# A four-layer graph network: row entries by distance, one-hot rows from TensorE, the attention's halves in banks of their own, and another order of the first pairs

## The chip, the cores and the metric

The kernel runs on one core of a Trainium2 chip. The metric is device time in microseconds (us) of one execution. The kernel before takes 883.4 us, the median of three runs (883.37 to 884.81).

The engines are named as in the profile: PE is TensorE's matmuls and PEld its weight loads, DVE is VectorE, ACT is ScalarE, POOL is GpSimd, and SP is SyncE, which here only issues DMAs. L12 means line 12 of the kernel before.

## The reference

The input `x` is 32 batch items of 512 nodes with 128 features, and `adj` is a 512 x 512 matrix in which about an eighth of the entries are non-zero. Four layers follow each other, each of them a layer norm, a relu, a graph layer, and a residual addition:

```python
# layer 0
h = relu(layernorm(x))
h0, h1 = h @ W[0], h @ W[1]
m = adj > 0
idx = cumsum(m.reshape(-1)) - 1            # number of the entry in row-major order
A = softmax(where(m, e[0][idx], NEG), axis=1)
x = x + (A * I) @ h0 + (A * (1 - I)) @ h1 + bias
# layer 1: Chebyshev hops (h A, 2 (h A) A - h) with A = adj, twice, then relu(cat @ Theta1 + b1)
# layer 2: (adj * adj)^T relu(h psi), phi1 with relu, phi2
# layer 3: A = exp(8 tanh(h q (h k)^T / (8 sqrt(128)))) * adj, rows normalised, A @ h @ v
```

The table `e` has 256 values, and an index beyond it takes the last of them. Only the first 256 entries of `adj`, which lie in its first few rows, therefore have a value of their own; all later ones share `e[255]`. The change lies wholly in layer 0.

## The kernel before

**Tiling.** A tile has 128 partitions (P). The 512 nodes are NT = 4 blocks t of 128. The batch is worked in 16 pairs q of two items b. NE = 256 entries of the table are NK = 2 blocks kk of 128. The kernel has eight PSUM banks of 128 x 512 f32, which `bank()` (L84) hands out in turn; a new use of a bank waits until the readers of the last one are done. For PE, DVE, ACT and POOL the kernel is traced with a manual schedule: each engine runs its instructions in the order of the program text, and only semaphores tie the engines together. So where a line stands among the lines of the same engine is where it runs. The Python generators in the text (`early_stats`, `normed_steps`, `turn_steps`, `project_steps`) give out one piece of work at each `next` or `go`, by which the pieces of one pair are woven in between those of others.

**The front end (L186 to L715)** makes the attention matrix A, while TensorE has little else to do.

- Masks `m` and the counts `rc` of each row come from DVE (L519), the additive mask `att` from POOL (L521). `p_incl` (L545) is the running count up to and with each row.
- Row entries (L553 to L560): for each block t, `of_row[row, e]` is 1 where entry e of the table falls in that row. DVE makes it as two compares: `lt` is e < incl, and `of_row` is (e >= before) times `lt`. TensorE sums it against `m` into `p_row` (L558).
- Place of each entry: `p_known` (L565) gives for each entry the row that it lies in and the count before that row; `p_upto` (L602) and the DVE compare with a sum, `scr_c` (L616), give its column.
- One-hot matrices of 0, 1 and values over (entry, node), which DVE makes by comparing `cols` with a column of numbers: `at_row` (L619), `at_col` (L620), and `at_part` (L623, the table's values split in three bf16 parts).
- `score_rows(t)` (L651): two matmuls subtract the first 256 entries from the mask (`p_later`), and six put their values into `p_val`.
- `softmax_rows(t)` (L663): DVE adds the mask (L665), reduces (L667), ACT takes the exponential (L668). `scaled_rows(t)` (L674): ACT scales by the reciprocal sum, POOL cuts out the diagonal (`diag`, L678) and subtracts it (L679, writes `att`).
- The attention is transposed by TensorE, `transpose_rows` (L482, shown as L485), into four banks `pt[j]`, one per block j of source nodes, where the target blocks t = 0, 1 are the first half of columns, and 2, 3 the second. `att_high`, `att_low`, `att_mid` (L372 to L391) split each half into three parts of 128 x 256 for the fp32r matmuls, one instruction for each j.

**A pair of layer 0** needs: statistics (`bn_stats` on DVE, then four small POOL instructions for pairs 0 to 2), eight relus `h` on ACT (L313), the turning of h to features-by-nodes `hT` (pairs 0 to 2 by TensorE, L331 and L596, and an ACT copy; from pair 3 on by DVE `hb`, L349, and a round of DMAs through DRAM), the product `p_g` with W[1] (L446, called from L455 on in `project_steps`) and its split g_high (ACT, L468), g_low (DVE, L470), g_mid (POOL L474 or DVE L472), and `hd`, hT times the diagonal of A (POOL, L728). Then TensorE adds, in two banks per pair: `own_sums` (L793, 16 matmuls with `hd`) and `mixed(q, I, part)` (L800, 48 matmuls in six groups of eight).

**Order around the change.** `first_sums()` (L810 to L858) weaves pair 0's sums with the turning, product and `hd` of pair 1, and with the turning of pair 2. `round0(q)` (L862) runs pairs 1 to 15: own sums, the product of pair q + 1, three mixed groups, the turning of pair q + 3, and three mixed groups. With q = 2 the split of pair 3's product (`go(steps)`, with g_low on DVE) stands after the first mixed groups and ahead of `turn(5)`.

Of the kernel before, what the change touches and what calls it, by code (L numbers as in the profile page):

```python
# [29 lines left out]
def kernel(  # L30
# [174 lines left out]
    known = prep.tile([P, NT, 2], F16, name="known")  # L205
    nc.vector.tensor_copy(known[:, :, 1], rows)
# [160 lines left out]
    def of_half(j, half):  # L367

        cols_of = slice(half * H, half * H + H)
        return pt[j][:, cols_of], [part[:, j, cols_of] for part in att_parts]  # L370
# [9 lines left out]
    def att_low(half):  # L380

        for j in range(NT):
            p, (high, low, mid) = of_half(j, half)
            nc.vector.tensor_sub(low, p, high.bitcast(F32))

    def att_mid(half):

        for j in range(NT):
# [61 lines left out]
    def bias(q):  # L450

        for b in range(2):
# [29 lines left out]
    def transpose_rows(banks, src, t):  # L482

        for j in range(NT):
            nc.tensor.transpose(banks[j][:, blk(t)], src[:, t, blk(j)], ident)  # L485
# [38 lines left out]

    pi = bank("p_incl")
# [16 lines left out]
    incl = prep.tile([P, NT], F32, name="incl")  # L542
    nc.vector.tensor_copy(incl, pi[:, :NT])
    before = prep.tile([P, NT], F32, name="before")
    nc.vector.tensor_sub(before, incl, rc)  # L545
# [6 lines left out]
    for t in range(NT):  # L552
        s = prep.tile([P, NE], F16, tag="lt", name=f"lt_{t}", bufs=2)  # L553
        nc.vector.tensor_scalar(s, cols[:, :NE], incl[:, t : t + 1], None, OP.is_lt)
        nc.vector.scalar_tensor_tensor(of_row[:, t, :], cols[:, :NE], before[:, t : t + 1], s,
                                       OP.is_ge, OP.mult)
# [4 lines left out]
    nc.vector.tensor_scalar(known[:, :, 0], before, float(NE), None, OP.min)  # L561
    pb = bank("p_known")[:, : 2 * NK].rearrange("p (k e) -> p k e", e=2)
    for kk in range(NK):
        for t in range(NT):
            nc.tensor.matmul(pb[:, kk, :], of_row[:, t, blk(kk)], known[:, t, :],  # L565
# [5 lines left out]
    row_of = prep.tile([P, NK], F32, name="row_of")  # L571
    nc.vector.tensor_copy(row_of, pb[:, :, 1])
    rest = prep.tile([P, NK], F32, name="rest")
    nc.vector.tensor_sub(rest, rows[:, :NK], pb[:, :, 0])
# [25 lines left out]
    for kk in range(NK):  # L600
        for j in range(NT):
            nc.tensor.matmul(pw[kk][:, j * P :], pgs[:, j, blk(kk)], upto[:, j, j * P :],  # L602
                             start=(j == 0), stop=(j == NT - 1), skip_group_check=True)
    turn_first(0)
    p_qk = bank("p_qk")
# [4 lines left out]
    at_row = prep.tile([P, NK, N], BF16, name="at_row")  # L610
# [7 lines left out]
    for kk in range(NK):  # L618
        nc.vector.tensor_scalar(at_row[:, kk, :], cols, row_of[:, kk : kk + 1], None, OP.is_equal)  # L619
# [89 lines left out]
    for j in range(NT):  # L709
        att_high(j, 0, j >= 2)  # L710
# [820 lines left out]
```

## Time and profile before

The profiled execution took 883.62 us, of which 881.8 are its span; the mean granted clock of TensorE was 0.997.

| stretch, us | PE busy | DVE busy | ACT busy | POOL busy | clock | DMA share |
|---|---|---|---|---|---|---|
| 0 to 30 (front end) | 24.55 | 25.66 | 14.12 | 18.99 | 1.00 | 0.80 |
| 30 to 80 (pairs 0 to 5) | 48.47 | 38.03 | 35.05 | 38.26 | 0.97 | 0.36 |
| 80 to 240 | 159.33 | 116.34 | 83.10 | 124.67 | 1.00 | 0.42 |
| 240 to 480 | 240.00 | 191.55 | 144.03 | 173.62 | 1.00 | 0.27 |
| 480 to 881.8 | 397.82 | 330.80 | 298.38 | 252.88 | 1.00 | 0.48 |

| instruction, 0 to 80 us | engine | mean ns of one |
|---|---|---|
| row entries `of_row`, 128 x 256 f16 | DVE | 484 |
| reduction L667, 128 x 512 | DVE | 692 |
| exponential L668, 128 x 512 | ACT | 722 |
| scaling L675, 128 x 512 | ACT | 718 |
| `att_high`, 128 x 256 | ACT | 382 |
| `att_low`, `att_mid`, 128 x 256 | DVE | 415, 417 |
| relu `h`, 128 x 128 | ACT | 485 |
| `hd`, 128 x 512 | POOL | 1290 |
| power L236 | POOL | 1426 |

A row names the engine's busy time in a stretch, or the mean duration of one instruction of a kind. A busy share averages over all of a stretch: an engine that is busy for half of it can still be the one that another engine waits for, since each works through its own queue in order. Which engine that is shows in the waits, where each idle time of an engine is put down to the instruction whose semaphore came last.

### The profile page before, as it was taken

Reading aid. Unit: us, or ns where it says so; the run is one execution under the profiler, and the core shown is the slowest. Engines: PE = TensorE matmul, PEld = TensorE weight load, DVE = VectorE, ACT = ScalarE, POOL = GpSimd, SP = SyncE. Lnnn points to the kernel's source line nnn. Section 1 sums busy time; section 2 is a strip of 40 time slices with the busy share of each in tenths; the row PEclk is TensorE's granted clock in tenths of the full one; section 3 lists DMA queues with packets and bytes.
Section 4 is the critical chain, followed back from the end, with each engine's and each line's share of the span. In section 5 each row is a group of like instructions: output and inputs, shape, how many; then the busy total and the mean of one; then the engine's idle time right before and its main releaser. Section 6 shows DMA issues by size and latency. Waiting matters only on the chain.

```text
span 881.8 us, 16286 instructions
## 1 busy us (share of the span) xinstructions
PE 870.2 (99%) x5520; PEld 771.3 (87%) x5520; DVE 702.4 (80%) x1428; ACT 574.7 (65%) x1279; POOL 608.4 (69%) x624
## 2 busy tenths in 40 slices
PE   8999999999999999999999999999999999999998
PEld 4799999988888888888888888888889988899987
DVE  8769877568587787888778888888789789988875
ACT  4765565355555656556666888875688788766674
POOL 5768988766777867867776566565476766677664
PEclk9999999999999999999999999999999999999999
DMA  9146664312322213122342445455445555555433
GB/s 262 29 133 182 194 186 120 97 49 73 101 68 73 72 48 96 49 72 72 97 120 77 116 134 136 138 152 146 134 123 141 157 156 159 151 143 147 128 100 86
DMA packets 107684, 103.91 MB, mean 118 GB/s; under 512 B 9552, under 2 KB 94160, under 8 KB 107600
## 3 DMA queue, kind: packets, MB, share of 16 engines
q1 hardware_dynamic: 107312, 102.34, 41.1%
q8 instruction: 44, 0.72, 0.4%
q10 hardware_dynamic: 288, 0.52, 0.2%
q14 instruction: 40, 0.33, 0.1%
HBM read 53.02 MB, written 49.81 MB: 117 GB/s over the span
## 4 chain that ended last, share of the span: by engine, by line
PE 90%; DVE 3%; ACT 2%; POOL 2%; DMA 1%; issue 1%; SPq 0%; POOLq 0%; ACTq 0%; DVEq 0%
PE p_av L1298 13%; PE p_l L990 10%; PE p_hidden L1194 10%; PE p_x1T L397 10%; PE p_score L1276 10%; PE p_l L800 8%; PE p_w L969 5%; PE p_l L446 3%; PE p_z L446 3%; PE p_w L971 3%; PE p_feat L1171 3%; PE p_hidden L1174 3%; PE p_g L446 2%; PE p_query L1230 2%; PE p_hv L1242 2%; PE p_l L793 2%
## 5 line engine op out<-in xcount | busy, mean ns | idle before, releaser
L1298 PEld LDWEIGHTS p_av<-hv,ex 128*128 128x128 f32 x1024 | 119.2, 191 | 3.0 <-POOL ex L1271 0.4
L1298 PE MATMUL p_av<-hv,ex 128*128 128x129 f32 x1024 | 119.7, 274 | 0.2 <-POOL ex L1271 0.2
L313 ACT ACTIVATE h<-x,sh,rs 128x128 f32<-128x128 f32 x256 | 102.9, 483 | 4.4 <-POOL sh L260 2.3
L427 POOL TENSOR_TENSOR key<-key 128x512 fp32r<-128x512 f32 x32 | 47.9, 1498 | 83.4 <-DVE key L426 66.5
L1271 DVE TENSOR_TENSOR ex<-ex,adjTx 128x512 f32<-128x512 f32 x64 | 79.0, 1237 | 32.4 <-ACT ex L1269 31.0
L1271 POOL TENSOR_TENSOR ex<-ex,adjTx 128x512 f32<-128x512 f32 x64 | 99.6, 1574 | 6.9 <-issue 3.5
L1100 ACT ACTIVATE h<-x,sh,rs 128x128 f32<-128x128 f32 x256 | 102.9, 485 | 0.0
L413 POOL TENSOR_TENSOR low_h<-h,high_h 128x512 fp32r<-128x512 f32 x32 | 55.3, 1732 | 45.6 <-PE p_w L971 26.3
L1277 ACT ACTIVATE ex<-p_score 128x512 f32<-128x512 f32 x128 | 76.2, 598 | 11.5 <-PE p_score L1276 4.7
L1269 ACT ACTIVATE ex<-ex 128x512 f32<-128x512 f32 x128 | 77.3, 634 | 0.0
L1158 POOL TENSOR_SCALAR high_hT<-hT 128x512 fp32r<-128x512 f32 x32 | 20.5, 641 | 56.0 <-PE p_hidden L1174 28.9
L246 DVE BATCH_NORM_STATS2 bn<-x 128x6 f32<-128x256 f32 x160 | 58.3, 419 | 0.0
L399 ACT COPY x1T<-p_x1T 128x512 f32<-128x512 f32 x32 | 18.8, 587 | 57.7 <-PE p_x1T L397 57.7
L1214 POOL TENSOR_TENSOR x<-x,phi2b 128x256 f32<-128x256 f32 x64 | 56.3, 900 | 0.0
L413 POOL TENSOR_TENSOR low_hs<-hs,high_hs 128x512 fp32r<-128x512 f32 x32 | 44.0, 1388 | 14.9 <-ACT high_hs L412 14.4
L1276 PE MATMUL p_score<-high_query,key 128*128 128x512 f32 x128 | 50.5, 394 | 0.0
L1276 PE MATMUL p_score<-mid_query,key 128*128 128x512 f32 x128 | 50.4, 394 | 0.0
L1276 PE MATMUL p_score<-low_query,key 128*128 128x512 f32 x128 | 50.4, 394 | 0.0
L431 ACT ACTIVATE high_query<-p_query 128x512 fp32r<-128x512 f32 x32 | 19.2, 600 | 46.5 <-PE p_query L1230 46.5
L971 PE MATMUL p_w<-th,x1T 128*128 128x128 f32 x256 | 49.0, 273 | 0.0
L414 DVE SCALAR_TENSOR_TENSOR mid_h<-h,high_h 128x512 fp32r<-128x512 f32 x32 | 27.7, 870 | 23.7 <-ACT high_h L412 16.2
L1109 DVE STREAM_TRANSPOSE hb<-h 128x512 f32<-128x512 f32 x64 | 43.5, 697 | 2.5 <-DMA d<-hb 1.9
(246 smaller groups left out, 2623.1 us busy)
## 6 DMA issues: line engine op xcount, KB each, us to landing
d<-hb SPq DMA_DIRECT2D x128, 128.0 KB, 2.4
hT<-d SPq DMA_DIRECT2D x32, 512.0 KB, 3.7
d_hT<-hb_hT SPq DMA_DIRECT2D x116, 128.0 KB, 2.4
hT<-d_hT SPq DMA_DIRECT2D x29, 512.0 KB, 3.3
x<-in_x_dram SPq DMA_DIRECT2D x32, 256.0 KB, 5.3
dv<-hvb SPq DMA_DIRECT2D x128, 64.0 KB, 1.8
hvt<-dv SPq DMA_DIRECT2D x32, 256.0 KB, 2.7
out_dram<-x SPq DMA_DIRECT2D x31, 256.0 KB, 2.5
```

The source lines that it names most:

```text
L313: nc.scalar.activation(h[:, b, t, :], xt[q][:, b, t, :], AF.Relu, bias=shift[q][:, i : i + 1], scale=scale[q][:, i : i + 1])
L397: nc.tensor.matmul(p, right[part][:, blk(t)], left[part][:, t, :], start=(t == 0 and part == 0), stop=(t == NT - 1 and part == 2))
L413: nc.gpsimd.tensor_sub(low, x, high.bitcast(F32))
L971: nc.tensor.matmul(p[:, D:], x1[q, b][:, blk(t)], th[:, 2, :], start=False, stop=True, skip_group_check=True)
L990: nc.tensor.matmul(p, adj_parts[part][:, t, blk(i)], w[r][part][:, t, :], start=(part == 0 and t == 0), stop=(part == 2 and t == NT - 1))
L1100: nc.scalar.activation(h[:, t, :], xt[q][:, b, t, :], AF.Relu, bias=shift[q][:, i : i + 1], scale=scale[q][:, i : i + 1])
L1194: nc.tensor.matmul(sums2[n], weighed_features[n][i][:, blk(t)], sq[i][:, t, :], start=False, stop=(i == 2 and t == NT - 1), skip_group_che ...
L1269: nc.scalar.activation(ex[:, t, :], ex[:, t, :], AF.Exp, scale=8.0)
L1271: eng.tensor_mul(split(ex[:, t, :]), split(ex[:, t, :]), crossed(mask[:, t, :]))
L1276: nc.tensor.matmul(p, keys[n][i][:, t, :], query[n][i], start=(i == 0), stop=(i == 2))
L1277: nc.scalar.activation(crossed(ex[:, t, :]), split(p), AF.Tanh, scale=UP / (8.0 * math.sqrt(D)))
L1298: nc.tensor.matmul(po[:, i, : D + 1], ex[:, t, blk(i0 + i)], hv[:, t, :], start=(t == 0), stop=(t == NT - 1))
```

## The change

It does seven things.

1. Row entries by distance. A row holds entry e when e is less than half its count away from the middle of its span. POOL makes `half` and `above` from the counts, DVE one small subtraction `middle`; ACT takes the absolute distance to `middle` (Abs with a bias by partition) for each t, and DVE makes one compare in place of two. `before` is computed after the loop, and `known` has one column.
2. One-hot rows by TensorE. `row_places(kk)` turns `of_row` with four matmuls against a 16-bit identity, and ACT copies the result to `at_row`. The DVE compares for `at_row` and the copy `row_of` go. `p_known` writes into free columns of `p_incl`'s bank.
3. g_mid of the second item of pair 0 by DVE in place of POOL.
4. `score_rows` is split into `later_rows` and `value_rows`, which are issued in another order; the statistics of pair 1, the turning of pair 0's second item and `bias(0)` move among them, and the last scaling goes behind an `att_high`.
5. The transposed attention has two banks for each half: `pt[half][j]` holds the blocks 2j and 2j + 1 of one half, and the three splits work on 128 x 512 elements, two instructions for a half in place of four.
6. Another order in `first_sums`: p_adiag right after the second transposes, the own sums of pair 0 earlier, all eight relus of pair 2 ahead of the split of pair 1's product, and the own sums of pair 1 (`begun`) at its end, ahead of the turning of pair 2 (the first seam). `round0(1)` takes them over.
7. In `round0`, `turn(q + 3)` moves ahead of the q == 2 branch (the second seam).

```diff
-    known = prep.tile([P, NT, 2], F16, name="known")
-    nc.vector.tensor_copy(known[:, :, 1], rows)
+    known = prep.tile([P, NT], F16, name="known")
     upto = prep.tile([P, NT, N], F16, name="upto")
...
-        cols_of = slice(half * H, half * H + H)
-        return pt[j][:, cols_of], [part[:, j, cols_of] for part in att_parts]
+        rows_of, cols_of = slice(2 * j, 2 * j + 2), slice(half * H, half * H + H)
+        return (pt[half][j].rearrange("p (t c) -> p t c", t=2),
+                [part[:, rows_of, cols_of] for part in att_parts])
...
-        for j in range(NT):
+        for j in range(2):
             p, (high, low, mid) = of_half(j, half)
...
-        for j in range(NT):
+        for j in range(2):
             p, (high, low, mid) = of_half(j, half)
...
-        for b in range(2):
+        for b in (1, 0):
             nc.gpsimd.tensor_add(xt[q][:, b], xt[q][:, b], spread(b0, NT))
...
-    def transpose_rows(banks, src, t):
-
+    def transpose_rows(t):
+
+        half, i = divmod(t, 2)
         for j in range(NT):
-            nc.tensor.transpose(banks[j][:, blk(t)], src[:, t, blk(j)], ident)
+            place = (2 * (j % 2) + i) * P
+            nc.tensor.transpose(pt[half][j // 2][:, place : place + P], att[:, t, blk(j)], ident)
...
+    half = prep.tile([P, NT], F32, name="half")
+    nc.gpsimd.tensor_scalar(half, rc, 0.5, None, OP.mult)
+    above = prep.tile([P, NT], F32, name="above")
+    nc.gpsimd.tensor_scalar(above, rc, 0.5, 0.5, OP.mult, OP.add)
+
     pi = bank("p_incl")
...
     go(early[0], 2)
-    incl = prep.tile([P, NT], F32, name="incl")
-    nc.vector.tensor_copy(incl, pi[:, :NT])
-    before = prep.tile([P, NT], F32, name="before")
-    nc.vector.tensor_sub(before, incl, rc)
+    middle = prep.tile([P, NT], F32, name="middle")
+    nc.vector.tensor_sub(middle, above, pi[:, :NT])
     h = {q: normed_tile(q) for q in range(3)}
...
         s = prep.tile([P, NE], F16, tag="lt", name=f"lt_{t}", bufs=2)
-        nc.vector.tensor_scalar(s, cols[:, :NE], incl[:, t : t + 1], None, OP.is_lt)
-        nc.vector.scalar_tensor_tensor(of_row[:, t, :], cols[:, :NE], before[:, t : t + 1], s,
-                                       OP.is_ge, OP.mult)
+        nc.scalar.activation(s, cols[:, :NE], AF.Abs, bias=middle[:, t : t + 1])
+        nc.vector.tensor_scalar(of_row[:, t, :], s, half[:, t : t + 1], None, OP.is_lt)
         for j in range(NT):
...
     go(early[0], 2)
-    nc.vector.tensor_scalar(known[:, :, 0], before, float(NE), None, OP.min)
-    pb = bank("p_known")[:, : 2 * NK].rearrange("p (k e) -> p k e", e=2)
+    before = prep.tile([P, NT], F32, name="before")
+    nc.vector.tensor_sub(before, pi[:, :NT], rc)
+    nc.vector.tensor_scalar(known, before, float(NE), None, OP.min)
+    at_row = prep.tile([P, NK, N], BF16, name="at_row")
+
+    def row_places(kk):
+        p = bank(f"p_at_row_{kk}")
+        for t in range(NT):
+            nc.tensor.matmul(p[:, blk(t)], of_row[:, t, blk(kk)], ident16, start=True, stop=True)
+        return p
+
+    p_row_0 = row_places(0)
+    pb = pi[:, NT : NT + NK]
     for kk in range(NK):
         for t in range(NT):
-            nc.tensor.matmul(pb[:, kk, :], of_row[:, t, blk(kk)], known[:, t, :],
+            nc.tensor.matmul(pb[:, kk : kk + 1], of_row[:, t, blk(kk)], known[:, t : t + 1],
                              start=(t == 0), stop=(t == NT - 1))
...
     nc.vector.tensor_copy(pgs[:, 2:4, :], pg[1])
-    row_of = prep.tile([P, NK], F32, name="row_of")
-    nc.vector.tensor_copy(row_of, pb[:, :, 1])
+    nc.scalar.copy(at_row[:, 0, :], p_row_0)
     rest = prep.tile([P, NK], F32, name="rest")
-    nc.vector.tensor_sub(rest, rows[:, :NK], pb[:, :, 0])
+    nc.vector.tensor_sub(rest, rows[:, :NK], pb)
     go(normal[0], NT - 2)
...
                              start=(j == 0), stop=(j == NT - 1), skip_group_check=True)
+    p_row_1 = row_places(1)
     turn_first(0)
+    nc.scalar.copy(at_row[:, 1, :], p_row_1)
     p_qk = bank("p_qk")
...
     col_of = prep.tile([P, NK], F32, name="col_of")
-    at_row = prep.tile([P, NK, N], BF16, name="at_row")
     at_col = prep.tile([P, NK, N], BF16, name="at_col")
...
     for kk in range(NK):
-        nc.vector.tensor_scalar(at_row[:, kk, :], cols, row_of[:, kk : kk + 1], None, OP.is_equal)
         nc.vector.tensor_scalar(at_col[:, kk, :], cols, col_of[:, kk : kk + 1], -1.0, OP.is_equal, OP.mult)
...
         nc.vector.scalar_tensor_tensor(low, high.bitcast(F32), -LOW, pg, OP.mult, OP.add)
-        nc.gpsimd.tensor_sub(mid, high.bitcast(F32), low.bitcast(F32))
+        if b:
+            nc.vector.scalar_tensor_tensor(mid, high.bitcast(F32), LOW + 1.0, pg, OP.mult, OP.subtract)
+        else:
+            nc.gpsimd.tensor_sub(mid, high.bitcast(F32), low.bitcast(F32))
...
-    def score_rows(t):
-        ph = scores[t]
+    def later_rows(t):
         for kk in range(NK):
-            nc.tensor.matmul(ph, at_row[:, kk, blk(t)], at_col[:, kk, :], start=False, stop=(kk == NK - 1))
+            nc.tensor.matmul(scores[t], at_row[:, kk, blk(t)], at_col[:, kk, :], start=False, stop=(kk == NK - 1))
+
+    def value_rows(t):
         pv = bank(f"p_val_{t}")
...
                                  stop=(kk == NK - 1 and i == 2))
-        scores[t] = ph, pv
+        scores[t] = scores[t], pv
...
     squares = turn_adj()
-    score_rows(0)
+    later_rows(0)
+    later_rows(1)
+    value_rows(0)
     next(project[0][0])
+    bias(0)
     softmax_rows(0)
     go(project[0][0])
-    score_rows(1)
-    go(early[1], 1)
-    turn_first(1)
-    bias(0)
+    later_rows(2)
+    value_rows(1)
     softmax_rows(1, lambda: inverse(0))
     scaled_rows(0)
-    score_rows(2)
-    go(early[1], 2)
-    score_rows(3)
+    go(early[1], 1)
+    later_rows(3)
+    value_rows(2)
+    turn_first(1)
+    value_rows(3)
...
     next(project[0][1])
-    inverted(3)
-    pt = [bank(f"p_attT_{j}") for j in range(NT)]
-    transpose_rows(pt, att, 0)
-    transpose_rows(pt, att, 1)
-    for j in range(NT):
-        att_high(j, 0, j >= 2)
+    go(early[1], 1)
+    inverse(3)
+    pt = [[bank(f"p_attT_{half}_{j}") for j in range(2)] for half in range(2)]
+    transpose_rows(0)
+    transpose_rows(1)
+    att_high(0, 0, False)
+    att_high(1, 0, True)
+    scaled_rows(3)
+    go(early[1], 1)
     go(project[0][1])
...
+    begun = {}
+
     def first_sums():
...
         mixed(0, 0, ps[0], 0, True)
-        transpose_rows(pt, att, 2)
-        transpose_rows(pt, att, 3)
-        for j in range(NT):
-            att_high(j, 1, True)
-        go(normal[1])
-        go(early[2], NT + 2)
-        att_low(1)
-        att_mid(1)
-        mixed(0, 0, ps[0], 1, True)
-        mixed(0, 0, ps[0], 2, True)
+        transpose_rows(2)
+        transpose_rows(3)
         p_adiag = bank("p_adiag")
...
             nc.tensor.matmul(p_adiag[:, blk(t)], ones, diag[:, t, :], start=True, stop=True)
+        att_high(0, 1, True)
+        att_high(1, 1, True)
         nc.scalar.copy(adiag[0], p_adiag)
-        go(early[2])
         diagonal_of(0, 0)
         diagonal_of(0, 1)
+        go(normal[1])
+        mixed(0, 0, ps[0], 1, True)
+        mixed(0, 0, ps[0], 2, True)
+        mixed(0, 1, ps[1], 0, True)
+        att_low(1)
+        mixed(0, 1, ps[1], 1, True)
+        go(early[2])
+        att_mid(1)
         next(turned[1])
-        mixed(0, 1, ps[1], 0, True)
         go(turned[1])
-        go(normal[2], NT)
-        go(ln3, NT)
+        own_sums(0, ps, False)
+        go(normal[2])
         next(project[1])
-        mixed(0, 1, ps[1], 1, True)
+        go(project[1])
         mixed(0, 1, ps[1], 2, True)
-        go(project[1])
-        go(normal[2])
-        go(ln3, 1)
-        own_sums(0, ps, False)
         diagonal_of(1, 0)
         diagonal_of(1, 1)
+        begun[1] = opened_sums(1)
+        own_sums(1, begun[1], True)
         bias(1)
-        go(ln3)
         for I in range(2):
...
         next(turned[2])
+        go(ln3)
         go(turned[2])
...
         both = stats_of_two(q - 1, q + 5) if q + 5 < NQ else stats_steps(q - 1, apart=True)
-        ps = opened_sums(q)
-        own_sums(q, ps, True)
+        ps = begun.pop(q, None)
+        if ps is None:
+            ps = opened_sums(q)
+            own_sums(q, ps, True)
         normal_of = normals.pop(q + 3, nothing)
...
             mixed(q, 0, ps[0], part, False)
+        if q + 3 < NQ:
+            go(turn(q + 3))
         if q == 2:
...
             bias(q + 1)
-        if q + 3 < NQ:
-            go(turn(q + 3))
         go(both, NT + 1)
...
```

## The prediction

> **What bounds the kernel now.** I read the page first, then the chain of waits, then each engine's instructions in order of time for 0 to 80 us, then busy time and granted clock by stretch. The page:
>
> ```profile
> span 881.8 us, 16286 instructions
> PE   8999999999999999999999999999999999999998
> PE 90%; DVE 3%; ACT 2%; POOL 2%; DMA 1%; issue 1%; SPq 0%; POOLq 0%; ACTq 0%; DVEq 0%
> ```
>
> TensorE carries 90% of the chain; only its first slice of 22 us has clear gaps. The chain in order of time shows where the other 10% lie:
>
> ```profile
> 39.87 1.30 POOL g_mid L474
> 41.17 1.97 POOL hd L728 x2
> ...
> 65.57 1.22 DVE hb_hT L349 x2
> ...
> 71.85 3.26 DMA hT<-d_hT
> ...
> 75.25 2.02 PE p_g L446 x16
> ```
>
> From 75.25 us on TensorE runs almost without a gap to the end: the waits listed for it after 70 us are this 1.2 us and four of 0.3 us or less. So the change, which touches only work up to there, is worth as much as it moves the start of this p_g (pair 5). It is bound by a DMA that starts with DVE's transpose of pair 5 at 65.57; TensorE's own work ahead of it ends at 74.0. Ahead of it, TensorE:
>
> ```profile
> 26.98 1.84 PE L800 MATMUL p_l<-g_high,att_high 128*128 128x256 f32 x8 [0.84 <-DVE att_high L378]
> 29.66 2.23 PE L485 MATMUL p_attT<-ident,att 128*128 128x128 f32 x8 [0.84 <-POOL g_mid L640]
> 43.48 2.03 PE L793 MATMUL p_l<-w,hd 128*128 128x128 f32 x16
> 47.05 1.20 PE L800 MATMUL p_l<-g_high,att_high 128*128 128x256 f32 x8
> ```
>
> Between 29.66 and 57.7 it has no gap, and the sums with hd of pair 1 start at 43.48, just as POOL ends hd (second line):
>
> ```profile
> 39.87 1.30 POOL L474 TENSOR_TENSOR g_mid<-g_high,g_low 128x512 fp32r<-128x512 f32 x1 [1.19 <-DVE g_low L470]
> 41.12 2.51 POOL L728 TENSOR_TENSOR hd<-hT,adiag 128x512 f32<-128x512 f32 x2
> ```
>
> The stretches give the clock (PEclk is third from the end):
>
> ```profile
> 29.00:30.00 1.00, 0.34 (x2) 0.24 (x2) 1.00 (x4) 0.00 (x0) 0.87 (x2) 1.00 0.02 8
> 30.00:31.00 1.00, 1.00 (x4) 0.66 (x5) 1.00 (x4) 0.00 (x0) 0.96 (x2) 0.54 0.00 0
> 32.00:33.00 1.00, 1.00 (x7) 1.00 (x7) 1.00 (x4) 1.00 (x4) 0.84 (x4) 0.50 0.00 0
> 33.00:34.00 1.00, 1.00 (x8) 1.00 (x8) 1.00 (x4) 1.00 (x4) 1.00 (x1) 0.76 0.00 0
> ```
>
> After 2.6 us of gaps between 25.2 and 29.66 the clock is halved for 3.4 us: 1.7 us of matmul time lost.
>
> **What the Trainium skill says.** "TensorE: Matmul & The Clock Gate", Part 1, What's actually happening: the array gets half its clock after an idle window of about 3.4 us, the full one after a busy window, and the windows run free. The trace agrees in length (3.4 us at 0.50), and shows that a window about a third used is enough. Same page, Part 2, Step-by-step: matmuls stay in program order, only weight loads are pulled ahead. So a matmul that waits holds up all behind it. "ScalarE: Activation LUTs", What ACT_TABLE_LOAD costs, prices an activation with a pointer bias at 280 ns + 0.833 ns per element, 93 ns less back to back; the relu of 128 elements (two pointers, 93 ns more) comes out at 0.48 us and 0.39 apart, and the trace has 0.44 and 0.40.
>
> **The change, part by part.** Times are us of the profiled span; I carried each engine's queue forward with the durations of these rows.
>
> Row entries. Removed: the cast of rows and the copy incl on DVE (0.07 each net) and four pairs of 0.72 (8.24 to 11.10). Added: half and above on POOL, 0.25 to 0.3 each behind att (ends 8.0), so middle runs at 8.56; on ACT four Abs of 0.40 (skill price, no such row; bounds 0.33, the att_high row of 256, and 0.5), behind the qkT copy (ends 8.9); on DVE four short compares. lt has two buffers, so the third Abs waits for the first compare. Last row: 10.93 instead of 11.10. But POOL's statistics start 0.5 later, the two relus before the pgs copy end at 11.8 instead of 11.36, so pgs on ACT goes from 11.57 to 11.8 and p_upto from 12.22 to 12.4.
>
> One-hot. Removed: two DVE compares of 0.265, at_part ends at 17.0 instead of 17.52. Added: eight short matmuls (0.8 in all) and two ACT copies of 0.53. The first copy stands before the relus that feed the hT copy: that goes from 13.96 to 14.5, p_g from 14.64 to 15.1. Then p_g 0.9, four later products 0.86 (two pulled ahead), six value products 1.30: done at 18.4. The first row's reduction starts at 18.4, as before (18.42). Net nothing; below that 0.6, where DVE's own 17.0 + 0.65 + 0.15 would bind; above it 0.4.
>
> Softmax order. One bn of 0.34 less per row on DVE, but the hT copy (0.53) now stands on ACT between the scalings of rows 0 and 1: exp of rows 1 to 3 start at 21.25, 23.8 and 25.6, against 21.59, 23.76 and 25.60. An att_high of 0.55 stands before row 3's scaling, so POOL's last own lies at 28.6 instead of 28.44. g_mid of block 1 goes from POOL (1.27) to DVE (0.6): pair 1's statistics start at 28.65 instead of 29.75.
>
> Banks. Transposes of the second half no longer wait for att_mid: 28.25 instead of 29.66. The 0.84 wait goes, and p_adiag moves up. Joined evictions cost about the same per element.
>
> Order of pairs 0 and 1. Now POOL's queue decides: statistics of pair 1 to 31.15, hd of pair 0 to 33.7 (adiag's copy ends at 30.75), statistics of pair 2 (2.45) to 36.15. ACT: pair 2's eight relus, 3.2, now stand whole before g_high of pair 1 (before, only four did): 36.2 to 39.4, g_high 39.95. DVE g_low 40.6, POOL g_mid 41.9, hd of pair 1 at 43.15 and 44.4. TensorE: from 28.25 it has 0.75 transposes, 0.9 adiag, four groups of 0.96 (some 0.3 waiting for DVE), 1.0 turning pair 1, 1.79 own sums, 1.79 p_g, 0.96: it is at hd of pair 1 at 39.2.
>
> First seam. The own sums of pair 1 are placed before the turning of pair 2, which is ready at 39.4 but stands behind them. TensorE waits 5.2 us, to 44.5. Then own sums 1.79, turning 0.9, copy and latency 0.4 (they overlap in halves), p_g 1.79: the mixed sums start at 49.35, against 47.05. The idle window halves the clock: with the phase of before it is cold from 43.7 to 47.1, 2.6 us of it used, 1.3 lost; other phases give 0.8 to 2.3. I take 1.4. So 50.75, 3.7 late.
>
> Second seam. DVE turns pair 5 before g_low of pair 3 and no longer waits for it: about 64 to 65 instead of 66.8 even with pair 3's relus waiting behind pair 2's copies on ACT. SP's queue order is unchanged: the four x loads still stand before these DMAs (2.08 of issue). The landing goes from 75.1 to about 74, and the 1.2 wait is gone; the wait of 0.29 at pair 3 (57.99) too, its data landing near 60.7 before TensorE comes at 61.2.
>
> Sum. 3.7 less 0.29 less 1.2 is 2.2 at pair 5; of that I give back 0.3, since the waits of 0.3 and less in layer 1 (0.68 between 183 and 204) can absorb part of a late arrival. Span 881.8 + 1.9 = 883.7; the profiled execution has 1.8 us around its span (883.62), so 885.5. The median shown is 883.4, 0.2 below that execution; I leave the 0.2 in, as it is within what the three runs scatter.
>
> **The rivals.** (1) The clock stays full, or is cold only while TensorE waits: the 3.7 is 2.3, and the sum 2.3 - 1.5 - 0.3, 0.5 late: 884.1. For it: the windows run free. Against: more than 4 us empty holds a third-used window at any phase. (2) Faster, by one mechanism: the front end is earlier than I make it. If the hT copy does not hold p_g back, ISA of row 0 runs at 17.8, and if the Abs and copies are cheaper in ACT's queue, the scaling chain follows DVE's pace of 1.85 a row instead of ACT's 2.2; last own 26.6, two us earlier, and, with half a us more saved among ACT's relus, hd of pair 1 at 41.9 and the mixed sums at 46.8 with the clock full. From the mixed sums on TensorE had 26.7 us of work to pair 5 in before (47.05 to 74.0, less the wait of 0.29): 73.5, 1.75 earlier than 75.25, so 881.7 from the median. It is faster at all from hd of pair 1 ending before 43.5 or so, and faster by 0.2% from 41.9. For it: DVE loses 1.6 us of work ahead of 25 us. Against: ACT gains 2.7. (3) Half way: hd of pair 1 ends at 43.4, one us earlier than in my count, and the clock is full: 0.5 - 1.0, so 883.1. (4) The half clock lasts 2 us longer over used time: 1.0 to 1.5 more, 887.
>
> **How the numbers follow.** My forecast 0.47 (885.5, own range 884.5 to 887), rival 1 0.15, rival 2 0.26, rival 3 0.06, rival 4 0.06. Rival 2 has that much because the three queues that meet in hd of pair 1 each carry an error of half a microsecond or more in my count. 0.2% (1.8 us) is about what a measurement of this kernel tells from no change. Below 881.6 lies the half of rival 2 in which the front end gains more than I priced, and a little of rival 3: 0.15; above 885.2 two thirds of my forecast (0.31) and rival 4: 0.37; between, 0.48. For 8 in 10: 881.3 to 887.0, which leaves out the lower third of rival 2 and the upper half of rival 4.
>
> **What would show it.** In the changed profile: last row entry near 10.9; p_g of pair 0 near 15.1; no wait for att_mid before the second transposes; own sums of pair 1 with a wait of some 5 us on POOL hd; clock 0.5 after it; mixed sums of pair 1 at 50 to 51; no DMA wait at pair 5. I am wrong if hd of pair 1 ends before 43, or if TensorE doesn't wait there.

## The result and the profile after

The changed kernel takes 885.25 us, the median of 19 executions (884.66 to 886.65), against 883.66 for the kernel before (19 executions, 883.29 to 884.81). The ratio is 1.0016, with a 95% interval of 1.0009 to 1.0023: 1.6 us slower, a small change whose interval leaves out 1. The profiled execution took 884.78 us, its span is 883.0 (before 881.8), and its mean clock 0.998.

The share of TensorE in the chain that ended last, from the page of the changed kernel:

```profile
span 883.0 us, 16282 instructions
...
PE 93%; POOL 2%; DVE 2%; ACT 2%; issue 1%; DMA 1%; SPq 0%; POOLq 0%; ACTq 0%
```

The chain in order of time, from 35 us on (start, duration, what):

```profile
35.81 3.19 ACT h L312 x8
39.00 0.49 ACT g_high L468
39.49 0.02 issue
39.52 0.70 DVE g_low L470
40.21 0.07 issue
40.28 1.27 POOL g_mid L474
41.55 2.46 POOL hd L752 x2
44.02 0.04 issue
44.06 3.29 PE p_l L817 x14
47.35 0.45 PE p_hT L330 x4
```

Before, this chain came back to TensorE at 75.25, through a DMA. Now it does so at 44.06 and stays there up to 80 us, but for one ACT copy of 0.59 at 47.82, with no DMA in between. Every piece ahead of 44.06 is one link of the queue that the prediction named: eight relus of pair 2, g_high, g_low, g_mid, then hd.

TensorE's instructions in order of time, where they differ (start, duration, instructions, and in brackets the idle time before them and what ended it):

```profile
26.81 1.22 PE L824 MATMUL p_l<-g_high,att_high 128*128 128x256 f32 x8 [1.47 <-DVE att_high L378]
27.87 1.03 PE L487 MATMUL p_attT<-ident,att 128*128 128x128 f32 x8
...
37.84 1.19 PE L824 MATMUL p_l<-g_mid,att_mid 128*128 128x256 f32 x8
42.83 0.49 PE L817 MATMUL p_l<-w,hd 128*128 128x128 f32 x2 [3.79 <-POOL hd L752]
44.06 3.29 PE L817 MATMUL p_l<-w,hd 128*128 128x128 f32 x14 [0.74 <-POOL hd L752]
47.19 1.04 PE L330 MATMUL p_hT<-ident,h 128*128 128x128 f32 x8
48.46 2.05 PE L446 MATMUL p_g<-w,hT 128*128 128x128 f32 x16 [0.24 <-ACT hT L333]
50.27 1.20 PE L824 MATMUL p_l<-g_high,att_high 128*128 128x256 f32 x8
...
74.75 1.95 PE L817 MATMUL p_l<-w,hd 128*128 128x128 f32 x16
76.54 1.95 PE L446 MATMUL p_g<-w,hT 128*128 128x128 f32 x16
```

The second transposes (L487) come at 27.87 instead of 29.66. By 39.0 TensorE has done all that it had done by 42.6 in the kernel before, 3.6 us ahead; then come the own sums of pair 1, and there it stands for 3.79 and 0.74 us. The mixed sums of pair 1 start at 50.27 instead of 47.05. At pair 5 (76.54) there is no wait. The busy time by stretch shows the clock (third from the end):

```profile
42.00:43.00 1.00, 0.17 (x1) 0.17 (x2) 1.00 (x3) 0.00 (x0) 1.00 (x2) 1.00 0.00 0
43.00:44.00 1.00, 0.32 (x2) 0.12 (x2) 0.94 (x3) 0.03 (x1) 1.00 (x2) 0.87 0.00 0
44.00:45.00 1.00, 0.94 (x4) 0.94 (x5) 0.69 (x3) 0.28 (x1) 1.00 (x2) 0.50 0.00 0
...
46.00:47.00 1.00, 1.00 (x7) 1.00 (x7) 0.00 (x0) 0.00 (x0) 0.87 (x3) 0.50 0.00 0
47.00:48.00 1.00, 1.00 (x10) 0.98 (x9) 0.00 (x0) 0.18 (x1) 0.00 (x0) 0.92 0.00 0
```

It is halved from 43.74 (a share of 0.26 at half clock makes the 0.87) to 47.16 (a share of 0.16 makes the 0.92), from the end of the stall on and over work that TensorE needs. The half clock that the kernel before had from 30 to 33.5 is gone, and TensorE's idle time there is one gap of 1.47 us now. That this is the reason is not shown: in the run with the banks alone, gaps of 0.29 and 1.11 us still end in a half clock.

For the waits at pairs 3 and 5, these are TensorE's lines of the kernel before:

```profile
56.59 1.12 PE L800 MATMUL p_l<-g_mid,att_mid 128*128 128x256 f32 x8
57.99 2.02 PE L446 MATMUL p_g<-w,hT 128*128 128x128 f32 x16 [0.29 <-DMA hT<-d_hT]
...
72.06 1.95 PE L793 MATMUL p_l<-w,hd 128*128 128x128 f32 x16
75.25 2.02 PE L446 MATMUL p_g<-w,hT 128*128 128x128 f32 x16 [1.24 <-DMA hT<-d_hT]
```

Start to start, the sum up to pair 5 is this. The mixed sums of pair 1 are 50.27 - 47.05 = 3.22 late. The wait at pair 3 is gone: a mixed group takes 0.96, so its p_g could have started at 56.59 + 0.96 = 57.55 and did at 57.99, and it ran 0.08 longer after the wait; 0.52 in all. The wait at pair 5 is gone: 72.06 + 1.79 = 73.85 against 75.25, 1.40. 3.22 - 0.52 - 1.40 = 1.30, and 76.54 - 75.25 is 1.29. The p_g of pair 5 also ran 0.08 longer behind its wait in the kernel before, so the group behind it starts 1.21 late (78.24 against 77.03). At the end of the span 1.2 is left.

### The profile page after: what moved, and what is told of

The parts are those of the page before. It is cut to its first block, busy times and chain, and to the rows that moved or that the text cites. A ratio compares the mean times of both kernels' runs of the same rounds, so it can differ in the third digit from the quotient of the medians.

```text
span 883.0 us, 16282 instructions
## 1 busy us (share of the span) xinstructions
PE 868.8 (98%) x5528; PEld 771.6 (87%) x5528; DVE 700.5 (79%) x1412; ACT 576.7 (65%) x1282; POOL 607.4 (69%) x625
## 4 chain that ended last, share of the span: by engine, by line
PE 93%; POOL 2%; DVE 2%; ACT 2%; issue 1%; DMA 1%; SPq 0%; POOLq 0%; ACTq 0%
PE p_av L1324 13%; PE p_l L1016 10%; PE p_hidden L1220 10%; PE p_x1T L397 10%; PE p_l L824 10%; PE p_score L1302 10%; PE p_w L995 5%; PE p_l L446 3%; PE p_z L446 3%; PE p_l L817 3%; PE p_g L446 3%; PE p_w L997 3%; PE p_feat L1197 3%; PE p_hidden L1200 3%; PE p_query L1256 2%; PE p_hv L1268 2%
## 5 line engine op out<-in xcount | busy, mean ns | idle before, releaser
L1297 DVE TENSOR_TENSOR ex<-ex,adjTx 128x512 f32<-128x512 f32 x64 | 79.4, 1243 | 32.1 <-ACT ex L1295 30.7
L432 DVE SCALAR_TENSOR_TENSOR z<-p_z,z 128x512 fp32r<-128x512 f32 x31 | 21.4, 691 | 30.3 <-ACT z L431 30.3
```

Source lines behind the costliest of these rows:

```text
L1297: eng.tensor_mul(split(ex[:, t, :]), split(ex[:, t, :]), crossed(mask[:, t, :]))
```

## The experiments

The experiments ran on two chips, the last two of the table on the second, and the kernel before takes 884.0 to 884.2 there against 883.66 above; so each time is given with its ratio to the kernel before measured with it. The changed kernel's is 1.0016 [1.0009, 1.0023]; it was not measured again beside them, so what is said of a run against it is a difference of two ratios. Two runs, e7 and e8, have five executions only, the others 13 to 21.

| run | median us | before | ratio [95% interval] |
|---|---|---|---|
| e1_own_back | 884.41 | 884.0 | 1.0002 [0.9994, 1.0011] |
| e2_hd_early | 882.62 | 884.0 | 0.9984 [0.9977, 0.9991] |
| e3_seam2_alone | 883.06 | 884.0 | 0.9988 [0.9982, 0.9995] |
| e4_clock_kept | 883.79 | 884.0 | 0.9997 [0.9989, 1.0005] |
| e5_no_seam2 | 886.63 | 884.16 | 1.0025 [1.0018, 1.0032] |
| e6_copies_first | 882.79 | 884.16 | 0.9981 [0.9975, 0.9988] |
| e7_stats_early | 878.6 | 884.16 | 0.9937 [0.9924, 0.995] |
| e8_old_front | 887.5 | 884.16 | 1.0033 [1.002, 1.0046] |
| e9_old_front_bias | 885.99 | 884.02 | 1.002 [1.0013, 1.0027] |
| e10_banks_alone | 883.54 | 884.02 | 0.9993 [0.9985, 1.0001] |

The theory at the start: TensorE waits for hd of pair 1, which POOL gives late because it is queued behind g_mid; the first seam puts the wait ahead of work that was ready; the clock is halved for it; the second seam takes the wait at pair 5. The main rival: hd is late for another reason, or the next wait lies right behind it, so that nothing is won by moving any of these.

### The first seam undone

```diff
-        begun[1] = opened_sums(1)
-        own_sums(1, begun[1], True)
```

> The changed kernel with the own sums of pair 1 back in round0(1), behind the turning of pair 2 (the first seam undone, all else kept). Theory A, TensorE stands still because own sums that wait for POOL's hd are placed ahead of a turning that is ready: the turning of pair 2 (0.87) runs at 39, the own sums still wait until 42.8 and 44.06, p_g of pair 2 follows at once, and the mixed sums of pair 1 start at 47.6 (clock full) to 48.8 (half clock), against 50.27: 1.5 to 2.7 us earlier, all of it kept at pair 5, whose data land near 74.5 - so 882.6 to 883.8 against 885.25. Rival B, the late hd of pair 1 sets the time wherever the own sums stand: mixed sums within 0.7 of 50.27, 884.6 to 885.3.

The ratio falls from 1.0016 to 1.0002, about 1.2 us, the upper end of theory A's range, though the two intervals overlap a little. In its profiled execution the turning of pair 2 fills the start of the stall, as theory A says (TensorE in order of time):

```profile
38.97 1.04 PE L330 MATMUL p_hT<-ident,h 128*128 128x128 f32 x8
42.92 0.79 PE L817 MATMUL p_l<-w,hd 128*128 128x128 f32 x2 [2.91 <-POOL hd L752]
44.14 3.36 PE L817 MATMUL p_l<-w,hd 128*128 128x128 f32 x14 [0.42 <-POOL hd L752]
47.29 2.79 PE L446 MATMUL p_g<-w,hT 128*128 128x128 f32 x16
49.83 1.20 PE L824 MATMUL p_l<-g_high,att_high 128*128 128x256 f32 x8
```

But the mixed sums start only at 49.83 there, later than theory A's 48.8: the clock was 0.5 from 42.2 to 49.0, twice as long as in the changed kernel, and p_g ran at half clock for a part too (2.79 instead of 2.05). The place of the own sums costs about a us; the order of POOL's queue, below, costs more.

### The clock held through the stall

```diff
+        p = bank("p_fill")
+        for i in range(30):
+            nc.tensor.matmul(p[:, : 2 * D], att_parts[0][:, i % NT, blk(0)],
+                             g[0][0][:, i % NT].rearrange("p b f -> p (b f)"), start=True, stop=True)
         begun[1] = opened_sums(1)
         own_sums(1, begun[1], True)
```

> The changed kernel with 30 matmuls that nothing reads (128 x 256, some 3.6 us) put on TensorE just ahead of the own sums of pair 1, into a bank of their own; they add nothing to the output. It fills the stall and leaves its end (44.06, POOL's hd) where it is. Theory A, the stall also costs the clock: the 3.4 us at 0.5 after it go, own sums and turning run at full speed, mixed sums at 48.4 to 48.9 instead of 50.27, 883.4 to 883.9 against 885.25, and the executions no longer differ in their mean clock (0.995 to 0.998 without it). Rival B, the half clock has another cause or hides under waits: 884.8 to 885.4.

```profile
38.74 3.76 PE L871 MATMUL p_fill<-g_high,att_high 128*128 128x256 f32 x30
42.73 0.49 PE L817 MATMUL p_l<-w,hd 128*128 128x128 f32 x2 [0.23 <-POOL hd L752]
43.95 1.83 PE L817 MATMUL p_l<-w,hd 128*128 128x128 f32 x14 [0.73 <-POOL hd L752]
```

(TensorE in order of time.) The 14 own sums take 1.83 instead of 3.29, and the mixed sums start at 48.70 instead of 50.27, 1.57 earlier. Of that, 0.11 is no work of the clock, as the second wait for hd ended at 43.95 instead of 44.06; from there to the mixed sums it is 4.75 instead of 6.21, so the half clock costs 1.46. The ratio falls by 0.0019, 1.7 us, and all 13 executions have a mean clock of 0.999 or 1.0. Theory A holds: 1.5 us of the loss at the seam are the clock's, and work that nobody reads makes the kernel faster. It also tells the size of the rest: with the clock held the changed kernel is even with the kernel before.

Two things are left open. In the profiled execution the lead over the changed kernel is 1.58 up to 104 us and 0.81 after a new wait of 0.54 for a DMA at 112.97; the spans differ by 0.6 (882.4 and 883.0). And the 13 executions still range from 883.32 to 885.10, so the clock is not all that makes executions differ.

### hd of pair 1 first on POOL

```diff
-        next(project[1])
-        go(project[1])
-        mixed(0, 1, ps[1], 2, True)
         diagonal_of(1, 0)
         diagonal_of(1, 1)
+        next(project[1])
+        go(project[1])
+        mixed(0, 1, ps[1], 2, True)
```

> The changed kernel with hd of pair 1 issued on POOL ahead of g_mid of pair 1 (only POOL's order moves). Theory A, hd of pair 1 is late only because it is queued behind a g_mid that waits for g_low, g_high and the eight relus of pair 2: POOL runs it from 35.8 to 38.3, TensorE comes at 39.0 and doesn't wait, the clock stays full, mixed sums of pair 1 at 44 to 44.5 instead of 50.27. Of the 6 us some 1.5 come back as a wait for the data of pair 3 (which hang on POOL's statistics of pair 3 and move only 4 to 4.5 us), so about 4.6 are left: 880.6, below the kernel before (883.66). Rival B, another wait takes its place at once (pair 2's turning or the parts of g of pair 1): mixed sums not before 47, 882 to 883.5. Rival C, POOL's queue only exchanges one late piece for another (g_mid of pair 1 late): 885.

The wait for hd goes entirely, and the ratio falls to 0.9984, below the kernel before. So the order of POOL's queue made hd late, as the theory says. But the gain is 2.8 us and not 4.6, and rival B names why: another wait, of 3.10 us, takes its place (TensorE, then ACT in order of time):

```profile
41.10 1.04 PE L330 MATMUL p_hT<-ident,h 128*128 128x128 f32 x8
45.23 3.49 PE L446 MATMUL p_g<-w,hT 128*128 128x128 f32 x16 [3.10 <-ACT hT L333]
```

```profile
40.42 1.28 ACT L254 ACT_TABLE_LOAD   x1
44.40 0.30 ACT L254 ACTIVATE sd<-bn,eps 128x8 f32<-128x8 f32 x1 [2.70 <-DVE bn L245]
44.61 1.05 ACT L333 COPY hT<-p_hT 128x512 f32<-128x512 f32 x2
```

ACT is idle for 2.70 us ahead of a small square root of pair 3's statistics, whose input DVE makes after its additions; the copies of pair 2's hT, which TensorE needs, stand behind it. In the changed kernel this wait was hidden behind hd. The clock is halved behind it too (3.49 for this p_g instead of 2.05), though not in every execution: the five with a mean clock of 1.0 took 880.90 to 881.88, the eleven with 0.998 took 882.31 to 882.94.

### The copies ahead of that square root

```diff
         next(turned[2])
-        go(ln3)
         go(turned[2])
+        go(ln3)
```

(on top of hd first)

> The kernel with hd early (e2_hd_early), and ACT's two copies of pair 2's hT ahead of the square root of pair 3's statistics. Theory A, the wait of 3.1 us that took hd's place there comes only from ACT's order (the copies stand behind a square root that waits for DVE's statistics, 44.4): the copies run at 41.7 to 42.7, p_g of pair 2 starts at 42.3 instead of 45.23 with the clock full, the mixed sums of pair 1 at 44.2 instead of 48.48. Pair 3's data land near 56.4 as before and give a wait of 1.5 to 2 at its p_g, so 2.2 to 2.7 are left: 1.5 to 2.7 us below e2_hd_early. Rival B, the next wait sits right behind (g of pair 1, or banks): mixed sums later than 46.5, less than 1 us gained.

Neither theory gave this. The mixed sums of pair 1 start at 43.58, even ahead of theory A's 44.2, but the time stays that of hd first alone. TensorE in order of time:

```profile
57.38 2.53 PE L446 MATMUL p_g<-w,hT 128*128 128x128 f32 x16 [3.14 <-DMA hT<-d_hT]
59.56 2.05 PE L824 MATMUL p_l<-g_high,att_high 128*128 128x256 f32 x8
```

The data of pair 3 land at 57.4 and no earlier, so TensorE stands for 3.14 us instead of the 1.5 to 2 expected, and the clock is halved again behind it (2.53 for a p_g, 2.05 for a mixed group). Of 4.9 us won at 43.58 (48.48 with hd first alone) nothing is left at pair 5 (74.78, against 74.74 with hd first alone).

### Pair 3's statistics early

```diff
         go(normal[2])
+        go(ln3, NT)
         diagonal_of(1, 0)
...
         own_sums(1, begun[1], True)
+        go(ln3)
         bias(1)
...
         next(turned[2])
-        go(ln3)
         go(turned[2])
```

(on top of hd first)

> The kernel of e6_copies_first with pair 3's statistics ahead: their DVE part in the idle stretch before g_low of pair 1 (35 to 39.5), their square root, reciprocal and shift right after g of pair 1 and ahead of bias(1) on POOL, the copies of pair 2 after them. Theory A: p_g of pair 2 starts near 42.6, the relus of pair 3 two us earlier (43.1), its data land near 54.3 before TensorE comes at 55: no wait at pair 3, mixed sums of pair 1 at 44.5, p_g of pair 5 near 71; 3.3 to 4 us below e2_hd_early and 1 to 1.7 below e6_copies_first, the lowest of all, near 879 on the chip where the kernel before takes 883.7. Rival B, pair 3 or 5 waits for its data all the same: within 0.6 of e6_copies_first.

878.6 us, ratio 0.9937 [0.9924, 0.995]: 5.6 us below the kernel before, and the lowest of all. Theory A holds at each step, with times some 0.5 to 0.9 us earlier than it said; the gain over the copies alone, 3.9 us by the ratios, is more than its 1 to 1.7, since that run had stayed short of its forecast. TensorE, from its last mixed group of pair 0 to p_g of pair 3:

```profile
37.80 1.20 PE L824 MATMUL p_l<-g_mid,att_mid 128*128 128x256 f32 x8
38.83 1.95 PE L817 MATMUL p_l<-w,hd 128*128 128x128 f32 x16
40.62 1.04 PE L330 MATMUL p_hT<-ident,h 128*128 128x128 f32 x8
42.06 2.05 PE L446 MATMUL p_g<-w,hT 128*128 128x128 f32 x16 [0.41 <-ACT hT L333]
43.87 1.20 PE L824 MATMUL p_l<-g_high,att_high 128*128 128x256 f32 x8
...
54.36 1.95 PE L446 MATMUL p_g<-w,hT 128*128 128x128 f32 x16
```

One gap of 0.41 is left in this stretch, the mean clock is 1.0 in all five executions, pair 3's data are there in time, and p_g of pair 5 starts at 70.14, 6.4 us ahead of the changed kernel. It is the changed kernel with a few lines in another place: three waits, set by the orders of POOL, ACT and DVE, lay one behind the other. How much of the gain needs the change's banks and seams, and how much the same lines would bring in the kernel before, no run shows.

### The second seam, alone and undone

```diff
         for part in range(3):
             mixed(q, 0, ps[0], part, False)
+        if q + 3 < NQ:
+            go(turn(q + 3))
         if q == 2:
             go(steps)
             bias(q + 1)
-        if q + 3 < NQ:
-            go(turn(q + 3))
```

(in the kernel before; undone in the changed kernel in the other run)

> The kernel before with the second seam alone: turn(q + 3) ahead of the q == 2 branch. Theory A, the wait at pair 5 hangs on DVE's transpose being queued behind g_low of pair 3: the transpose ends near 62.5 to 63 instead of 66.8, the data land near 72.3, TensorE's own work ends at 73.85, so the wait of 1.24 (1.40 from start to start) goes: 882.2 to 882.4 against 883.66. Rival B, the landing is set by the x loads that share the queue and the DMA engines: wait still over 1.0, 883.4 to 883.8.

> The changed kernel with the second seam undone (turn(q + 3) behind the q == 2 branch again). Theory A, the data of pair 5 land some 2.2 us later than in the kernel before, near 77.3, since DVE's queue is shifted by so much, and TensorE now comes at 76.54: a wait of 0.7 to 0.9 at pair 5 and 0.6 to 0.9 us more time than the changed kernel; the seam is worth less here than in the kernel before (1.4), as a late TensorE waits less. Rival B, the seam is worth the full 1.4 here too. Rival C, nothing, TensorE is late enough: within 0.2 of the changed kernel.

Alone it brings the ratio to 0.9988, 1.0 us faster, and the wait at pair 5 is gone. TensorE in order of time, in the kernel before with the seam, then in the changed kernel without it:

```profile
72.96 1.95 PE L793 MATMUL p_l<-w,hd 128*128 128x128 f32 x16
74.74 1.95 PE L446 MATMUL p_g<-w,hT 128*128 128x128 f32 x16
```

```profile
75.22 1.95 PE L817 MATMUL p_l<-w,hd 128*128 128x128 f32 x16
78.50 1.69 PE L446 MATMUL p_g<-w,hT 128*128 128x128 f32 x13 [1.33 <-DMA hT<-d_hT]
```

With the seam, own sums and p_g are at their plain distance of 1.79. This execution lost some 0.9 more to the half clock before 36 us, so TensorE comes later than in the kernel before; but the DMA for pair 5 starts at 70.36 instead of 71.85 all the same. Rival B, a landing set by the x loads, is out. Undone in the changed kernel it costs 0.8 us by the ratios (1.0025 against 1.0016, intervals that overlap), as theory A has it, but in the profiled execution the wait at pair 5 is 1.33 in brackets and 78.50 - 75.22 - 1.79 = 1.49 from start to start, nearer to rival B's 1.4. Between those two it stays open; the wait itself, which the changed kernel doesn't have, speaks against rival C, that the seam is worth nothing there.

### The old front end in the changed kernel

The row entries and one-hot rows as before (parts 1 and 2 of the change undone), the rest as changed.

> The changed kernel with its row entries and one-hot rows made as in the kernel before (two compares on DVE for each block, at_row by DVE), everything after it as changed. Theory A, the new front end nets nothing: hd of pair 1 ends within 0.4 of 44.06, time within 0.5 of the changed kernel. Rival B, it was worth 1 us or more, since DVE loses 1.6 us of work: hd of pair 1 past 45. Rival C, it costs time, as ACT gains 2.7 us of work: hd of pair 1 before 43.4.

The time is higher by 0.0017, 1.5 us, and the second wait for hd ends 1.3 later (45.37 instead of 44.06): rival B, on its face. But the instructions of the one-hot values (kind, count, least, median and longest ns) show something else:

```profile
L626 DVE TENSOR_SCALAR at_part<-cols,col_of,part x6: 409/410/1359, 15.8 to 17.4; 128x512 bf16<-128x512 f16 x6
```

One of six takes 1.36 us instead of 0.41. It starts at 17.37, while POOL runs the first addition of `bias(0)`, which the change had moved ahead of the first row's softmax and which starts here at 17.15. So one more run with `bias(0)` back in its old place:

```diff
     next(project[0][0])
-    bias(0)
     softmax_rows(0)
...
     value_rows(1)
+    bias(0)
     softmax_rows(1, lambda: inverse(0))
```

> The kernel with the old front end (e8_old_front), and bias(0) on POOL back ahead of the second row's softmax, where it no longer meets DVE's at_part. In e8_old_front one at_part took 1.36 us instead of 0.41 while POOL's bias(0) ran. Theory A, of the 1.3 us by which e8_old_front's hd of pair 1 was later than the changed kernel's, 0.95 are that collision and the front end itself is worth 0.3 to 0.4: all six at_part take 0.41, hd of pair 1 ends at 44.3 to 44.7, time 0.7 to 1.1 us below e8_old_front. Rival B, the front end is worth the 1.3 by itself: hd at 45.2 or later, time as e8_old_front. Rival C, bias(0) costs as much in its new place, since POOL's cuts of the diagonal wait for it: at_part 0.41, but hd past 45.

All six now take 0.41 to 0.42, and the second wait for hd ends at 44.17, 0.1 later than in the changed kernel. The ratio is 1.002, 0.0004 (0.4 us) above the changed kernel's and inside its interval. Theory A is right that the collision was most of it: 1.20 of the 1.31 us at hd are gone with it. The front end itself is worth 0.1 us at hd, less than the 0.3 to 0.4 I had left for it. (TensorE also waits 0.45 us for pair 3's data in this execution, which it doesn't in the changed kernel; the reason is not shown.)

### The banks alone in the kernel before

The transposes and splits of part 5, in the order of the kernel before.

> The kernel before with part 5 alone: two banks for each half of the transposed attention and the three splits on 128 x 512 elements, the order of all else as before. Theory A, the second transposes come 1.4 to 1.8 us earlier (wait for att_mid gone), no half clock near 30 to 33.5, p_adiag and the turning of pair 1 some 2.5 to 3 us earlier, and the chain adiag, hT, relus, g_high, g_low, g_mid, hd of pair 1 moves with them by 1 to 2 us until POOL's statistics hold it: mixed sums of pair 1 at 45 to 46 instead of 47.05; but the waits at pairs 3 and 5 grow by part of it: 0.5 to 1.5 us faster than before. Rival B, TensorE's gain ends in a longer wait for hd of pair 1, which POOL gives no earlier: within 0.4 of before. Rival C, the pieces of 512 elements delay the first mixed sums (both halves of a split instead of one at a time): 0.5 or more slower.

0.9993 [0.9985, 1.0001], 0.5 us below before and not clear of no change, so between theory A and rival B by its size. The trace is rival B's. The second transposes come at 28.87 instead of 29.66 and p_adiag at 33.18 instead of 34.40. But ACT copies adiag at 35.42, practically where it did before (35.55), since eight relus of pair 1 stand ahead of it; hd of pair 1 starts at 41.02 instead of 41.12. The half clock is still there, from 28.7 to 32.1. In the changed kernel p_adiag's copy stands ahead of the relus and starts at 29.84; that the banks gain TensorE time only with this order fits, but no run has that order alone.

## Why the prediction was right

The forecast was 885.5, slower through the first seam, and 885.25 was measured. Its mechanism held at the seam: TensorE waited for hd of pair 1, and its sign of being wrong, an hd that ends before 43, did not come (44.01). By its steps:

- **Front end, net nothing.** Right: the first row's reduction starts at 18.21 (18.4 said, 18.42 before), the last row entry ends at 11.06 (10.93 said), and undoing it moves hd by 0.1 us. What I did not see is the collision of DVE and POOL that it escaped by a hair (last section). One reading was wrong: the relu of 128 elements takes 0.485 us in the kernel before, and the relus follow each other at 0.39 (eight take 3.19), not 0.44 and 0.40; so the trace is nearer to the skill's price than I wrote. An Abs took 0.44 (four take 1.77), inside its bounds.
- **Banks and transposes at 28.25.** Right within 0.4: 27.87.
- **POOL's queue decides, hd of pair 1 at 43.15 and 44.4.** Right within 0.4: 42.78 and 44.01. POOL's statistics of pair 1 start 0.42 ahead of the count (28.23 against 28.65), which accounts for it. The runs with hd first on POOL show that this order is the cause and not only its place in the chain.
- **TensorE stands for 5.2 us from 39.2.** 3.79 + 0.74 = 4.5 us from 39.0, on either side of two own sums that the first hd had released (0.49). Those two sums and hd's slightly earlier end are the difference. The turning of pair 2 stood behind them, as said: it starts at 47.19, and at 38.97 with the seam undone.
- **Half clock costs 1.4.** It is 1.46 by the filled stall. Rival 1, no cost, is out. The Trainium skill ("TensorE: Matmul & The Clock Gate", Part 1, What's actually happening) says that the windows run free, and the trace agrees: the clock fell at 43.74, 4.7 us after TensorE's last matmul, and in the run without the second seam at 42.04, 3.1 us after it, for the same stall. So it is luck that the profiled execution has the very edges of the forecast, 43.7 and 47.1.
- **3.7 late at the mixed sums.** 3.22, so 0.5 less.
- **Waits at pairs 3 and 5, 0.29 and 1.2.** Their mechanism held, and their sizes were too small: I took the idle time in brackets, which leaves out a slow start behind a wait; from start to start they are 0.52 and 1.40, and 1.48 with the slow p_g behind the second.
- **0.3 given back in layer 1.** Wrong: nothing was. TensorE is 1.21 late when layer 1 starts (184.88 against 183.67) and 1.2 late at the end of the span. The waits there stayed as they were (0.30 for low_h in both kernels): what TensorE waits for came later by as much as TensorE.

So the profiled execution was forecast 0.7 too slow: 1.2 in the span, where I had 1.9. That is 0.48 at the mixed sums and 0.51 at the two waits, less the 0.30 of layer 1. The median came closer because that execution was one of the faster ones, and that much of the closeness is luck. Of 19 executions the six with a mean clock of 0.998 took 884.66 to 884.99, the others, with 0.995 or 0.996, 885.01 to 886.65. The profiled execution without the second seam has the same stall and 0.996: its clock is 0.5 from 42.04 to 48.9, two windows instead of one, the turning of pair 2 runs at half clock too, and its mixed sums start at 50.64 instead of 50.27. That fits a second cold window in those executions; no trace of the changed kernel itself shows one. From the second hd to the mixed sums, the stall is followed by 6.21 us in the changed kernel and 4.75 with the clock held; in the other three runs with the same stall it is 6.69 (e5), 6.84 (e9) and 7.19 (e8). So the half clock costs 1.46 to 2.44, and the bounds of 0.8 to 2.3 that I gave for other phases were a little too narrow.

Rival 2 needed hd of pair 1 before 41.9. That wasn't so in the changed kernel; in the run with hd first it ended at 38.7, and the kernel was then faster, though the next wait kept the gain to 2.8 us.

## What to carry over

Where engines run in program order, price a moved step by the queue that it waits for. Here TensorE reaches the own sums of pair 1 at 39, and they wait for POOL's hd, which could have run at 36 but stood behind a g_mid that was late. After a wait is removed, list what else was due by then (a copy, statistics, a DMA) before adding up a gain; here three removals in a row were worth 2.8, 0.3 and 3.9 us. An idle stretch of TensorE costs its own length and then the clock over the work behind it: here 4.5 us of standing and 1.5 to 2.4 more, as the halved stretch falls differently from execution to execution.

## What the runs showed of the hardware

A DVE instruction that reads and writes 16-bit numbers in SBUF (at_part, 0.41 us) took 1.36 us in e8_old_front when it started at 17.37, 0.22 after a POOL addition had begun. The Trainium skill ("SBUF — State Buffer", SBUF: two separate sides) describes an exclusive lock on a port pair that some DVE instructions share with POOL's, held by the first of the two for its whole instruction. The trace agrees in kind: the 0.95 us lost are most of what was left of POOL's addition, which by its record ended at 18.58. The mask addition behind it ran beside POOL's second addition in its usual 0.74, so not every DVE instruction is held up. In the changed kernel the last at_part ends at 17.04 and `bias(0)` starts at 17.05. By an estimate from that one collision, a DVE queue some 0.4 us later, so that this at_part starts behind `bias(0)`, would pay about 0.95.

The clock fell though TensorE was far from idle. In the kernel before, in the 3.41 us ahead of the fall (26.67 to 30.08), TensorE was busy for 2.25, and no gap in it was longer than 0.84. In the changed kernel 2.13 of the 3.42 us up to 40.33 were busy, and the clock stayed full. So the stretch ahead of the fall need not be idle, unlike the idle window that the prediction quotes, and busy time alone does not tell when the clock falls; these runs do not settle what does.

A clock once halved did not return after 3.4 us that were used in most part: in e1_own_back TensorE was busy for 2.29 of the 3.41 us from 42.22 on, and the clock stayed at 0.5 up to 49.0. It was back after 3.4 us in the kernel before, where TensorE was busy throughout, and in the changed kernel, where it was busy for 3.10 of 3.42.
